# Routing in eleven slot-sized pieces, GpSimd work issued a slot later, input copies shared by two engines, and a regrouped end, in a gated cross-attention and mixture-of-experts kernel

## The chip, the cores and the metric

The kernel runs on one core of a Trainium2 chip. The core has five engines that work side by side, each through its own instructions in order: TensorE (PE in the profile) multiplies matrices, VectorE (DVE) and GpSimd (POOL) do elementwise work and reductions, ScalarE (ACT) does activations and copies, and SyncE (SP) issues most of the DMAs. They wait for one another through semaphores. The metric is the time of one execution on the device in microseconds (us), as the median of several runs. A profiled execution gives a trace of every instruction; its span runs from the first to the last instruction of the program.

## What is computed

```python
# x: 32 x 112 x 256, ctx: 32 x 375 x 256, all float32; 16 heads of 64; 8 experts, 2 of them per token
def attention(ctx, lat, ln_m_g, ln_m_b, ln_l_g, ln_l_b, Wq, Wkv, Wout):
    c = layer_norm(ctx, ln_m_g, ln_m_b)
    l = layer_norm(lat, ln_l_g, ln_l_b)
    q = l @ Wq                                        # 256 -> 1024
    k, v = split(concatenate([c, l], axis=1) @ Wkv)   # 487 keys
    attn = softmax(q @ k.T * 64 ** -0.5)              # for each batch and head
    return (attn @ v) @ Wout

def experts(x, gate_w, w1, b1, w2, b2):
    s, idx = top_k(softmax(x @ gate_w), 2); s = s / sum(s)
    y = gelu(x @ w1 + b1) @ w2 + b2                   # hidden size 1024, for each expert
    return sum over the two chosen experts of s * y

x = x + tanh(g_xattn) * attention(ctx, layernorm(x), ...)
x = x + tanh(g_ffn) * experts(layernorm(x), ...)
```

## The kernel before

**Attention, in 128 steps.** The 32 batches are taken in pairs. A step is one batch and two pairs of heads, so a pair of batches takes eight steps, m = 0 to 7; I call these eight a block, 0 to 15. Keys and values of a pair of batches come from a scheme of seven products instead of eight (`seven`, lines 341 to 418): four products (`p1`, `p6`, `p7`, `p5`) are copied from PSUM by ScalarE and summed by GpSimd (line 383), three more are added by VectorE (line 409).

A step n (lines 1034 to 1191) first runs `attend` of an earlier pair of steps on TensorE if n is even, then `scores(n + 1)` on TensorE with two maxima on VectorE (line 445, `nmx`), then five slots h = 0 to 4. In a slot TensorE gets one or two of the seven products or a query projection, then `turn_attn(n, h)` transposes a quarter of the attention weights, and VectorE copies it out of PSUM (line 481, `exT`). Behind that VectorE gets the slot's small work from a list `dve[h]`; the softmax's exponentials and its division (`exps`, `norm`) are on ScalarE, with a reciprocal on VectorE (line 468) before the division. All engines' orders are fixed by the order in which this Python code issues the instructions. PSUM banks for everything but scores come from a pool of four (`ps_m`), so TensorE runs at most four results ahead of the engines that empty them.

**What rides along.** Layer norm of a coming batch: statistics on VectorE (`stat`, line 218), roots on GpSimd (lines 237 to 246), application on ScalarE, all from `ln_parts`; then `turn` transposes the inputs on TensorE, and two ScalarE activations for each half copy them out with gain and offset (line 288), or VectorE does so for the first two batches (line 292). When a slab of 128 tokens is complete, `project`, `residual`, `normed` and `logits_of` give its output projection, residual sum, norm and eight gate logits (lines 517 to 569). Where a slab's number u is 0, these fall on steps m = 0, 2 and 3, where it is 1 on m = 0, 1, 4 and 5. Block 0 has no slab, the blocks 1, 5, 9 and 13 have one (u = 1), all others two.

**Routing.** Slabs form eight groups, six of four slabs and two of two. A step after a group's last logits, `route_parts` is issued: `first_choice` in slot 1, `second_choice` and `tanh` in slot 2, `counts` in slot 3; a step later `places` (two small matmuls into `ps_pos`, lines 629 and 632) in slot 0, with `gates`, and `slots_of` in slot 1. Then each token row is scattered to its expert's place in the table `xg` by indirect DMAs on GpSimd's queue (line 661), one a slot. For group 0, eight `stranger_hits` and `stranger_ids` come in between. Groups 0 to 5 end in the steps 27, 45, 61, 83, 99 and 117, group 6 in step 125, group 7 after the loop.

**Experts.** 60 blocks of 128 rows, which are fetched from `xg` in the order of the experts: `turn_rows` transposes, `hidden` is the first layer with Gelu on ScalarE, `second` the second layer, `combine` adds the bias on VectorE, scales, and scatters with addition on GpSimd's queue (line 910). The first ones run inside the last two steps and in the lines 1194 to 1238, from line 1256 on a plain loop. `locate_early` and `locate_late` compute on VectorE which rows each block takes.

## Time and profile before

| | before |
|---|---|
| median of 3 runs | 2220.05 us (2218.36 to 2221.41) |
| profiled execution | 2220.04 us |
| its span | 2218.3 us |
| TensorE busy | 2154.6 us |
| ScalarE, VectorE, GpSimd busy | 1296.7, 1229.0, 1015.3 us |
| mean granted TensorE clock | 0.991 |
| attention (first scores to last) | 20.1 to 1746.6 us |

A profile's line of a group or of the timeline gives start, duration, engine, source line, operation, what is written and read, shape, and in brackets the idle time before it and the instruction that ended it. TensorE's busy time includes small waits, as the ends of its pipelined matmuls are modelled; the distance between the starts of the same matmul in two steps does not have this fault.

### The profile page before, as it was taken

The numbers are of one execution on the slowest core, as the hardware profiler recorded it, in microseconds if no ns is written. First come the engines' busy times: TensorE is split into PE (matmuls) and PEld (weight loads), VectorE is DVE, ScalarE is ACT, GpSimd is POOL, SyncE is SP. The second block draws the span as 40 slices with busy tenths as digits, with TensorE's granted clock in tenths as the row PEclk, the third lists the DMA queues.
The fourth block names the chain that finished last, engine by engine and source line by source line (L and its number), as shares of the span: only waits on it lengthen the run. The fifth ranks groups of instructions, "written<-read, shape, count | busy, mean of one in ns | idle before, by whom it ended". The sixth has DMA issues, their size and how long they took to land. (4 is left out here: it accounts for less than half of the span.)

```text
span 2218.3 us, 42154 instructions
## 1 busy us (share of the span) xinstructions
PE 2154.6 (97%) x15944; PEld 1672.6 (75%) x15944; DVE 1229.0 (55%) x2698; ACT 1296.7 (58%) x3075; POOL 1015.3 (46%) x1388
## 2 busy tenths in 40 slices
PE   8999999999999999999999999999999899999998
PEld 5777767676777676777776777677767789999998
DVE  5566676767666767665667666756676541111111
ACT  5666666556666666667665666576655534344343
POOL 5745454455456544654545454555445232122122
PEclk9999999999999999999999999999999999999999
DMA  6592000010001000100000000000002236755453
GB/s 144 174 325 88 17 13 18 3 41 15 15 13 36 13 17 13 39 8 15 13 17 32 17 13 26 20 15 4 9 11 72 93 83 189 211 160 158 127 147 69
DMA packets 113701, 138.21 MB, mean 62 GB/s; under 512 B 14704, under 2 KB 101432, under 8 KB 113368
## 3 DMA queue, kind: packets, MB, share of 16 engines
q1 hardware_dynamic: 101032, 119.11, 17.3%
q0 software_dynamic: 11328, 15.33, 3.8%
q8 instruction: 127, 2.08, 0.4%
q10 hardware_dynamic: 1136, 1.05, 0.2%
q14 instruction: 78, 0.64, 0.1%
HBM read 166.84 MB, written 48.99 MB: 97 GB/s over the span
## 5 line engine op out<-in xcount | busy, mean ns | idle before, releaser
L470 ACT ACTIVATE ex<-ex,rc 112x487 f32<-112x487 f32 x512 | 331.7, 697 | 288.7 <-DVE rc L468 287.8
L445 DVE TENSOR_REDUCE nmx<-ps_s 112x2 f32<-112x974 f32 x256 | 287.3, 1163 | 346.3 <-PE ps_s L435 346.3
L456 ACT ACTIVATE ex<-ps_s,nmx 112x487 f32<-112x487 f32 x512 | 337.5, 667 | 167.5 <-DVE nmx L445 119.8
L481 DVE COPY exT<-ps_t 122x448 f32<-122x448 f32 x512 | 315.9, 617 | 105.8 <-PE ps_t L477 105.2
L477 PEld LDWEIGHTS ps_t<-ident,ex 112*122 112x122 f32 x2048 | 233.1, 139 | 138.5 <-issue 73.4
L887 ACT ACTIVATE h<-ps_h,b 128x128 f32<-128x128 f32 x480 | 175.6, 367 | 260.5 <-PE ps_h L880 220.1
L477 PE MATMUL ps_t<-ident,ex 112*122 112x112 f32 x2048 | 285.6, 262 | 17.7 <-ACT vv L403 7.3
L435 PE MATMUL ps_s<-kT,qT 64*112 64x487 f32 x1024 | 242.0, 591 | 0.0
L910 POOL DMA_INDIRECT out_dram<-y,xs x60 | 93.7, 1561 | 318.1 <-DVE y L909 189.2
L880 PE MATMUL ps_h<-xsT,w 128*128 128x128 f32 x1920 | 229.4, 277 | 4.8 <-ACT xsT L871 1.6
L880 PEld LDWEIGHTS ps_h<-xsT,w 128*128 128x128 f32 x1920 | 227.2, 194 | 9.1 <-issue 3.1
L491 PEld LDWEIGHTS ps_o<-exT,vv 122*64 122x64 f32 (+1 forms) x4096 | 197.7, 136 | 44.7 <-DVE rc L468 20.1
L893 PE MATMUL ps_y<-w,h 128*128 128x256 f32 x960 | 217.0, 379 | 0.0
L383 POOL TENSOR_TENSOR tmpv<-vv,tmpv 122x512 f32<-122x512 f32 x64 | 81.4, 1271 | 292.1 <-ACT tmpv L393 291.9
L491 PE MATMUL ps_o<-exT,vv 122*64 122x112 f32 (+1 forms) x4096 | 211.5, 260 | 0.0
L383 POOL TENSOR_TENSOR vv<-tmpv,vv 122x512 f32<-122x512 f32 x128 | 165.6, 1294 | 98.9 <-ACT vv L403 62.0
L373 PE MATMUL ps_v<-wkv_s,tT 128*122 128x128 f32 x1536 | 202.8, 275 | 0.2
L367 PE MATMUL ps_k<-tT,wkv_s 128*128 128x487 f32 x378 | 193.3, 594 | 4.7 <-ACT tmpk L393 3.2
L893 PEld LDWEIGHTS ps_y<-w,h 128*128 128x128 f32 x960 | 177.9, 190 | 21.8
L373 PEld LDWEIGHTS ps_v<-wkv_s,tT 128*122 128x122 f32 x1536 | 182.6, 186 | 2.2 <-issue 0.6
L373 PEld LDWEIGHTS ps_v<-wkv,kvT 128*122 128x122 f32 x1024 | 125.8, 185 | 74.3 <-issue 70.7
L409 DVE TENSOR_TENSOR kT<-ps_k,kT 128x487 f32<-128x487 f32 x189 | 124.8, 660 | 87.6 <-PE ps_k L367 80.1
(202 smaller groups left out, 3371.7 us busy)
## 6 DMA issues: line engine op xcount, KB each, us to landing
w<-in_L_ffn_w_dram SPq DMA_DIRECT2D x120, 1024.0 KB
xg<-pad SPq DMA_DIRECT2D x8, 3640.0 KB
cin<-in_ctx_dram SPq DMA_DIRECT2D x32, 336.0 KB
xs<-xg SPq DMA_DIRECT2D x60, 130.0 KB
b<-in_L_ffn_b_dram SPq DMA_DIRECT2D x60, 128.0 KB
xin<-in_x_dram SPq DMA_DIRECT2D x32, 112.0 KB
x<-in_x_dram SPq DMA_DIRECT2D x28, 128.0 KB
out_dram<-x SPq DMA_DIRECT2D x28, 128.0 KB
```

The lines of the kernel that those rows point to most:

```text
L367: nc.tensor.matmul(ps, lhsT=w[:, 0, i * P : (i + 1) * P], rhs=x[:, :NK], start=True, stop=True)
L373: nc.tensor.matmul(ps[:, c, :], lhsT=x[:, c * KC : (c + 1) * KC], rhs=w[:, 1, i * P : (i + 1) * P], start=True, stop=True,)
L383: nc.gpsimd.tensor_tensor(v[o], v[l], v[r], ALU.add)
L435: nc.tensor.matmul(ps[:, j, :NK], lhsT=qT[b // 2, i][r, b % 2, :], rhs=kT[b, i][r, :], start=True, stop=True,)
L445: nc.vector.tensor_reduce(nmx[b, i], pss[b, i][:, :, :NK], AX.X, ALU.max, negate=True)
L456: nc.scalar.activation(t[:, j, :NK], ps[:, j, :NK], AF.Exp, bias=nmx[b, i][:, j : j + 1], accum_out=sm[b, i][:, j : j + 1],)
L470: nc.scalar.mul(ex[b, i][:, j, :NK], ex[b, i][:, j, :NK], rc[:, j : j + 1])
L477: nc.tensor.transpose(ps[:, c, :], ex[b, i][:, j, c * KC : (c + 1) * KC], ident[:S, :S])
L481: nc.vector.tensor_copy(exT[b, i, j], ps)
L491: nc.tensor.matmul(ps[y * DH : (y + 1) * DH, r, x * S : (x + 1) * S], lhsT=vv[j][:m, c, x, r, y * DH : (y + 1) * DH], rhs=exT[2 * g + x, i ...
L880: nc.tensor.matmul(ps, lhsT=w1t[:, k, f * P : (f + 1) * P], rhs=xsT[t][:, k, :], start=(k == 0), stop=(k == KD - 1),)
L893: nc.tensor.matmul(psy[t], lhsT=hid[t][:, f, :], rhs=w2t[:, f, :], start=(f == 0), stop=(f == NF - 1),)
```

## The change

Routing becomes eleven parts (`choice` in six, `both`, `counts`, `places`, `gates`, `slots_of`), and from two slots after the last logits one part is issued in each slot. The `place` sum moves from `slots_of` to `gates`. GpSimd's roots and its copies of rows and token numbers are not issued at once but collected in `soon_` and issued after the next slot's `turn_attn`. The iota `slot` moves to another pool, and the four buffers of the exponentials become fixed tiles whose padding is zeroed once, not 256 times. Of the two halves of a turned input, ScalarE copies one out and VectorE the other. Batch statistics move from steps 7 and 1 to steps 6 and 7, and the application on ScalarE by one slot. At the start, weight sums are issued in another order. At the end the last products for K and V are spread over the steps 123 to 125 instead of 124 and 125, `turn_rows(0)` moves to the end of step 125 (and its copy to the pool `early`), the first hidden products of block 0 are cut otherwise, the counts are made a step later, and the order after the loop changes. Line numbers below are those of the text, not of the profile.

```diff
...
     wo_sb = wp.tile([P, NP, D], F32, name="wo_sb")
+    soon_ = []
+    outgoing = []
...
             stat(st[:S], mv[:S], CC, xin[b][:, 0, :])
+            soon_.append(roots)
+        def roots():
             gp = nc.gpsimd
...
+    exs = [[const.tile([S, 2, NKP], F32, name=f"ex_{n}_{p}") for p in range(2)] for n in range(2)]
+    for n in range(2):
+        for p in range(2):
+            nc.gpsimd.memset(exs[n][p][:, :, NK:], 0.0)
     def heads_of(n):
...
         ps = pss.pop((b, i))
-        t = soft.tile([S, 2, NKP], F32, tag="ex", name=f"ex_{b}_{i}", bufs=4)
-        nc.gpsimd.memset(t[:, :, NK:], 0.0)
+        t = exs[n % 2][p]
         sm[b, i] = soft.tile([S, 2], F32, tag="sm", name=f"sm_{b}_{i}", bufs=4)
...
         stat(st, mvx[i], 0, x1[i])
-        ve = small.tile([P, 1], F32, tag="vex", name=f"vex_{i}")
-        nc.gpsimd.tensor_scalar(ve, mvx[i][:, 0, 1:2], EPS, None, ALU.add)
-        rsx[i] = small.tile([P, 1], F32, tag="rsx", name=f"rsx_{i}")
-        nc.gpsimd.tensor_tensor(rsx[i], ve, nhalf[:, :1], ALU.pow)
+        def root():
+            ve = small.tile([P, 1], F32, tag="vex", name=f"vex_{i}")
+            nc.gpsimd.tensor_scalar(ve, mvx[i][:, 0, 1:2], EPS, None, ALU.add)
+            rsx[i] = small.tile([P, 1], F32, tag="rsx", name=f"rsx_{i}")
+            nc.gpsimd.tensor_tensor(rsx[i], ve, nhalf[:, :1], ALU.pow)
+        soon_.append(root)
...
         )
-        nc.gpsimd.tensor_copy(xr[g][:, j, 1, :D], xr[g][:, j, 0, :D])
+        soon_.append(lambda: nc.gpsimd.tensor_copy(xr[g][:, j, 1, :D], xr[g][:, j, 0, :D]))
...
-    def first_largest(src, n, g):
+    def first_largest(src, n, g, found):
         mx = rt.tile([P, src.shape[1]], F32, tag=f"mx{n}", name=f"mx{n}_{g}")
-        nc.vector.tensor_reduce(mx, src, AX.X, ALU.max)
         at = rt.tile([P, src.shape[1], E], F32, tag=f"sel{n}", name=f"sel{n}_{g}")
-        nc.vector.tensor_tensor(at, src, over_e(mx), ALU.is_equal)
-        nc.vector.tensor_tensor(at, at, over_b(rank, src.shape[1]), ALU.mult)
         top = rt.tile([P, src.shape[1]], F32, tag=f"top{n}", name=f"top{n}_{g}")
-        nc.vector.tensor_reduce(top, at, AX.X, ALU.max)
-        nc.vector.tensor_tensor(at, at, over_e(top), ALU.is_equal)
-        return mx, at
-    outgoing = []
+        found[f"m{n}"], found[f"s{n}"] = mx, at
+        def largest():
+            nc.vector.tensor_reduce(mx, src, AX.X, ALU.max)
+            nc.vector.tensor_tensor(at, src, over_e(mx), ALU.is_equal)
+        def where_first():
+            nc.vector.tensor_tensor(at, at, over_b(rank, src.shape[1]), ALU.mult)
+            nc.vector.tensor_reduce(top, at, AX.X, ALU.max)
+        def first():
+            nc.vector.tensor_tensor(at, at, over_e(top), ALU.is_equal)
+        return [largest, where_first, first]
...
-        def first_choice():
-            v["m1"], v["s1"] = first_largest(logits, 1, g)
-        def second_choice():
-            rest = new("rest", [P, RG, E])
-            nc.vector.scalar_tensor_tensor(rest, v["s1"], -BIG, logits, ALU.mult, ALU.add)
-            v["m2"], v["s2"] = first_largest(rest, 2, g)
+        choice = first_largest(logits, 1, g, v)
+        new("rest", [P, RG, E])
+        choice += first_largest(v["rest"], 2, g, v)
+        first, second = choice[2], choice[5]
+        def rest():
+            first()
+            nc.vector.scalar_tensor_tensor(
+                v["rest"], v["s1"], -BIG, logits, ALU.mult, ALU.add
+            )
+        def apart():
+            second()
...
+        choice[2], choice[5] = rest, apart
+        def both():
+            nc.scalar.activation(v["th"], v["th"], AF.Tanh, scale=0.5)
+            nc.vector.tensor_tensor(new("both", [P, RG, E]), v["s1"], v["s2"], ALU.add)
+            nc.vector.tensor_copy(new("had", [P, RG, E])[:, 0, :], macc)
         def counts():
-            both = new("both", [P, RG, E])
-            nc.vector.tensor_tensor(both, v["s1"], v["s2"], ALU.add)
-            had = new("had", [P, RG, E])
-            nc.vector.tensor_copy(had[:, 0, :], macc)
+            both, had = v["both"], v["had"]
             for j in range(1, RG):
...
-        def tanh():
-            nc.scalar.activation(v["th"], v["th"], AF.Tanh, scale=0.5)
         def gates():
+            place = new("place", [P, RG, E])
+            nc.vector.tensor_tensor(place, v["ps"], over_b(eoff, RG), ALU.add)
+            if g == 0:
+                strangers()
             half = new("half", [P, RG])
...
             for k in range(2):
-                nc.gpsimd.tensor_copy(
-                    xr[g][:, :, k, D + 1].bitcast(I32), tok[:, b0 : b0 + RG]
+                soon_.append(
+                    lambda k=k: nc.gpsimd.tensor_copy(
+                        xr[g][:, :, k, D + 1].bitcast(I32), tok[:, b0 : b0 + RG]
+                    )
                 )
...
         def slots_of():
-            place = new("place", [P, RG, E])
-            nc.vector.tensor_tensor(place, v["ps"], over_b(eoff, RG), ALU.add)
+            place = v["place"]
             slot = new("slot", [P, 2, RG])
...
-        pads = strangers, stranger_hits, stranger_ids, strangers_out
-        if g == 0:
-            return first_choice, second_choice, tanh, counts, places, gates, slots_of, pads
-        return first_choice, second_choice, tanh, counts, places, gates, slots_of
+        parts = choice + [both, counts, places, gates, slots_of]
+        return parts, (stranger_hits, stranger_ids, strangers_out)
...
-    (f0, t0), (f1, t1), (ln_now, ln_then) = (ln_parts(b) for b in range(3))
+    then = {}
+    (f0, t0), (f1, t1), (ln_now, then[2]) = (ln_parts(b) for b in range(3))
...
             part()
+    def now():
+        while soon_:
+            soon_.pop(0)()
...
     do(f0)
+    now()
     nc.vector.tensor_copy(lnT, ps)
...
         k_plain(0, i)
+    weight_sums(0, 1)
     do(f1)
-    weight_sums(0, 1)
+    now()
     do(t1)
...
     norm(0, 0)
-    weight_sums(1, 0)
+    do(ln_now)
+    now()
     ahead, behind = {}, {}
...
     do(ahead[0, 1][1:])
-    do(ln_now)
+    weight_sums(1, 0)
...
         none = [lambda: None] * 4
-        if n < LAST - 4:
-            one, two = ((1, jv), (0, jk))[odd], ((0, jk), (1, jv))[odd]
-            one, two = ahead.get(one, none), behind[two]
+        one, two = ((1, jv), (0, jk))[odd], ((0, jk), (1, jv))[odd]
+        one, two = ahead.get(one, none), behind.get(two, none)
+        if n < LAST - 5:
             slots = [[two[0], one[0]], [two[1]], [one[1], two[2]], [one[2]], [one[3]]]
...
-            slots = [[], [], [], [], []]
-            if n == LAST - 4:
-                for slot_, unit in zip(slots, behind[0, jk]):
-                    slot_.append(unit)
-            if n < LAST - 2:
-                j = LAST // 2 - 2 + odd
+            for j in (LAST // 2 - 2, LAST // 2 - 1):
                 if (1, j) not in ahead:
                     ahead[1, j], behind[1, j] = seven(1, j)
-                one, two = ahead[1, j], behind[1, j]
-                for slot_, units in zip(slots, (one[:2], one[2:3], one[3:], two[:2], two[2:])):
-                    slot_ += units
+            (p1, p6, p7, p5), (p2, p4, p3) = ahead[1, LAST // 2 - 2], behind[1, LAST // 2 - 2]
+            (q1, q6, q7, q5), (q2, q4, q3) = ahead[1, LAST // 2 - 1], behind[1, LAST // 2 - 1]
+            slots = {
+                5: [[two[0], one[0]], [two[1], one[1]], [two[2], p1], [one[2], p6], [one[3]]],
+                4: [[two[0], p7], [two[1], p5], [two[2], p2], [p4, q1], [p3, q6]],
+                3: [[q7], [q5], [q2], [q4], [q3]],
+            }.get(LAST - n, [[], [], [], [], []])
...
                 for h in range(4):
-                    dve[h].append(ln_then[h])
+                    dve[min(h + 1, 3)].append(then[nb + m // 2][h])
             if m == 1:
-                pe[1] += [lambda k=k: turn(nb, k) for k in range(KD)]
-                ln_now, ln_then = ln_parts(nb + 1)
+                pe[1] += [lambda: turn(nb, 0), lambda: turn(nb, 1, nc.vector)]
             if m == 3:
-                pe[1] += [lambda k=k: turn(nb + 1, k) for k in range(KD)]
+                pe[1] += [lambda: turn(nb + 1, 0), lambda: turn(nb + 1, 1, nc.vector)]
             if m == 4:
...
                     dve[h].append(part)
-            if m == 7 and nb + 2 < B:
-                ln_now, ln_then = ln_parts(nb + 2)
-            if m == 1 or (m == 7 and nb + 2 < B):
+            if m in (6, 7) and nb + 2 < B or n == 1:
+                u = m - 4 if m > 1 else 1
+                ln_now, then[nb + u] = ln_parts(nb + u)
                 for h in range(4):
...
             i = ended(2 * g - 2 + u) if g > 0 else None
-            if m == 6 + u and ended(2 * g + u) is not None and g + 1 < B // 2:
+            if m == 6 + u and ended(2 * g + u) is not None:
                 load_slab(ended(2 * g + u))
...
                 if group[i][1] == groups[group[i][0]] - 1:
-                    due, todo = n + 1, group[i][0]
-        if n == due:
-            r = route_parts(todo)
-            dve[1].append(r[0])
-            dve[2] += r[1:3]
-            dve[3].append(r[3])
-        if n == due + 1:
-            pe[0].append(r[4])
-            dve[0].append(r[5])
-            if todo > 0:
-                dve[1].append(r[6])
-            else:
-                far, hits, ids, ids_out = r[7]
-                dve[1].append(far)
-                at = [(j, e) for j in range(2) for e in range(0, E, 2)]
-                extra = [[lambda: None]]
-                for k in range(len(at) + 1):
-                    extra.append([lambda p=p: ids(*p) for p in at[k - 1 : k] if k > 0])
-                    extra[-1] += [lambda p=p: hits(*p) for p in at[k : k + 1]]
-                extra += [[ids_out], [r[6]]]
-        if n == LAST - 9:
+                    r, (hits, ids, ids_out) = route_parts(group[i][0])
+                    extra = [[], []] + [[part] for part in r[:10]]
+                    if group[i][0] == 0:
+                        at = [(j, e) for j in range(2) for e in range(0, E, 2)]
+                        for k in range(len(at) + 1):
+                            extra.append([lambda p=p: ids(*p) for p in at[k - 1 : k] if k > 0])
+                            extra[-1] += [lambda p=p: hits(*p) for p in at[k : k + 1]]
+                        extra.append([ids_out])
+                    extra.append(r[10:])
+        if n == LAST - 8:
             pe[0].append(lambda: found.update(ps=counted()))
...
             dve[1].append(lambda: next(early))
-        if n == LAST - 8:
+        if n == LAST - 7:
             for h in range(3):
...
             fetch_weights(0)
+        if n == LAST - 3:
+            pe[4].append(lambda: turn_rows(0))
         if n == LAST - 2:
-            pe[0] += [lambda: others(ends), lambda: turn_rows(0)]
-            pe[1] += [lambda: hidden(0, 0, 2)]
-            pe[2] += [lambda: hidden(0, 2, 4)]
-            pe[3].append(lambda: hidden(0, 4, 6))
-            pe[4] += [lambda: hidden(0, 6, 8), lambda: turn_rows(1, nc.scalar.copy)]
+            pe[0] += [lambda: others(ends), lambda: hidden(0, 0, 1)]
+            pe[1] += [lambda: hidden(0, 1, 3)]
+            pe[2] += [lambda: hidden(0, 3, 5)]
+            pe[3].append(lambda: hidden(0, 5, 7))
+            pe[4] += [lambda: hidden(0, 7, 8), lambda: turn_rows(1, nc.scalar.copy)]
         if n == LAST - 1:
...
             turn_attn(n, h)
+            then_ = soon_[:]
+            del soon_[:]
+            do(then_)
             for part in dve[h]:
...
     i, g = TS - 2, len(groups) - 1
-    while outgoing:
-        outgoing.pop(0)()
-    for u in range(2):
-        load_slab(i + u)
+    while extra:
+        do(extra.pop(0))
+    now()
+    do(outgoing)
+    del outgoing[:]
     attend(LAST // 2 - 1)
-    hidden(2, 0, 1)
+    hidden(2, 0, 2)
     for u in range(2):
...
     residual(i)
+    now()
     second(0)
     residual(i + 1)
+    now()
     normed(i)
-    hidden(2, 1, 2)
+    now()
+    logits_of(i, 0, 4)
+    hidden(2, 2, 8)
     normed(i + 1)
-    logits_of(i, 0, E)
+    now()
+    logits_of(i, 4, E)
     biased(0)
+    fetch_weights(3)
     logits_of(i + 1, 0, E)
-    fetch_weights(3)
-    first_choice, second_choice, tanh, counts, places, gates, slots_of = route_parts(g)
     turn_rows(3, nc.scalar.copy)
-    hidden(2, 2, 5)
-    first_choice()
-    second_choice()
-    tanh()
-    hidden(2, 5, 8)
-    counts()
+    r, _ = route_parts(g)
+    do(r[:7])
     second(1)
-    places()
+    fetch_weights(4)
+    r[7]()
+    second(2)
+    fetch_weights(5)
+    r[8]()
     found["ps"] = counted()
-    gates()
-    slots_of()
-    while outgoing:
-        outgoing.pop(0)()
+    r[9]()
+    now()
+    r[10]()
+    do(outgoing)
     locate_late()
...
     combine(1)
-    fetch_weights(4)
     for t in range(NE, NE + AHEAD):
...
     turn_rows(4)
-    second(2)
     combine(2)
-    fetch_weights(5)
...
```

More of the change, by code (lines that the diff above doesn't have):

```diff
@@ L138 @@
     nc.vector.tensor_copy(tokf, tok[:, :2])
-    slot = const.tile([P, P], F32, name="slot")
-    nc.gpsimd.iota(
-        slot, pattern=[[1, P]], base=0, channel_multiplier=0, allow_small_or_imprecise_dtypes=True
-    )
     row = const.tile([P, 1], F32, name="row")
@@ L192 @@
         b1rows = wqp.tile([E * NF, P], F32, name="b1rows")
+        slot = wqp.tile([P, P], F32, name="slot")
+        nc.gpsimd.iota(
+            slot,
+            pattern=[[1, P]],
+            base=0,
+            channel_multiplier=0,
+            allow_small_or_imprecise_dtypes=True,
+        )
         wq_sb = wqp.tile([P, KD, INNER], F32, name="wq_sb")
@@ L644, in gates @@
                 for k in range(2):
-                    nc.gpsimd.tensor_copy(
-                        xr[g][:, :, k, D + 1].bitcast(I32), tok[:, b0 : b0 + RG]
+                    soon_.append(
+                        lambda k=k: nc.gpsimd.tensor_copy(
+                            xr[g][:, :, k, D + 1].bitcast(I32), tok[:, b0 : b0 + RG]
+                        )
                     )
             def slots_of():
-                place = new("place", [P, RG, E])
-                nc.vector.tensor_tensor(place, v["ps"], over_b(eoff, RG), ALU.add)
+                place = v["place"]
                 slot = new("slot", [P, 2, RG])
@@ L869, in turn_rows @@
                 nc.tensor.transpose(ps[:, k, :], xs[t][:, k * P : (k + 1) * P], ident)
-            xsT[t] = found["tiles"].tile([P, KD, P], F32, tag="xsT", name=f"xsT_{t}")
+            xsT[t] = found["tiles" if t > 0 else "early"].tile(
+                [P, KD, P], F32, tag="xsT", name=f"xsT_{t}"
+            )
             (copy or nc.vector.tensor_copy)(xsT[t], ps)
@@ L1032 @@
         sums_at = {0: (0, 2), 1: (1, 1), 2: (0, 3), 3: (1, 2), 4: (0, 0), 5: (1, 3)}
-        filled, due, extra = 0, LAST, []
+        filled, extra = 0, []
         for n in range(LAST):
```

## The prediction

> **What bounds it now.** I read the page's busy shares first, then TensorE's windows block by block, its waits, and the timelines of the engines that it waits for.
>
> ```profile
> PE 2154.6 (97%) x15944; PEld 1672.6 (75%) x15944; DVE 1229.0 (55%) x2698; ACT 1296.7 (58%) x3075; POOL 1015.3 (46%) x1388
> ```
>
> TensorE has work 97% of the time and the change gives it none less. Only its waits, and the slow clock after them, can be won. The next windows cut the span at the first score matmul for each block of eight steps, which the step before it issues (columns: stretch, length, TensorE busy, granted clock, DMA share, GB/s); then come single steps.
>
> ```profile
> 220.92:327.94 107.02, 105.90 (x809) 1.00 0.05 15
> 327.94:447.61 119.67, 113.56 (x837) 0.97 0.03 10
> ...
> 992.18:1094.29 102.11, 101.61 (x793) 1.00 0.05 15
> 1094.29:1208.61 114.32, 109.31 (x814) 0.97 0.06 20
> ```
>
> ```profile
> 302.69:317.63 14.94, 14.45 (x125) 1.00 0.01 1
> ...
> 1176.90:1198.29 21.39, 17.45 (x129) 0.84 0.02 7
> ```
>
> A plain block takes 107.0 us (102.1 with one slab). Blocks with routing take more: block 3 12.65, 4 4.2, 6 5.5, 8 4.5, 10 7.3, 11 0.9, 12 7.1, 13 0.5; and step 119 7.1 more than its like (20.58 against 13.50). Sum 49.8. The pair of steps shows how: 6.45 us more, 3.45 of it idle and 3.4 (0.16 of 21.39) lost to a slow clock, less a little work.
>
> ```profile
> PE ps_pos L629 <- DVE had L619: 2.0, 1, 2.0
> PE ps_t L477 <- ACT vv L403: 1.4, 1, 1.4
> ```
>
> These are TensorE's waits around that step: the position matmul waits for the last instruction of `counts`, and a transpose for a PSUM bank that ScalarE frees late because it sat behind `tanh`. The timeline says why VectorE was late:
>
> ```profile
> 1177.79 1.21 POOL L322 TENSOR_TENSOR tT<-kvT 128x488 f32<-128x488 f32 x1
> 1177.91 1.14 DVE L583 TENSOR_TENSOR sel<-sel,rank 128x32 f32<-128x32 f32 x1
> ...
> 1180.42 1.27 POOL L383 TENSOR_TENSOR vv<-tmpv,vv 122x512 f32<-122x512 f32 x1 [1.42 <-ACT vv L398]
> 1180.47 1.49 DVE L560 CUSTOM_DVE_ANT_0 junk<-xr,gw_sb 128x256 f32<-128x256 f32 x1
> ```
>
> Alone, these two take 0.19 and 0.42 us; beside a GpSimd add they last as long as the add. Two more places, the start and the end:
>
> ```profile
> 37.51 0.60 ACT L250 ACTIVATE cin<-cin,sh,rsc 125x256 f32<-125x256 f32 x1 [3.72 <-POOL sh L246]
> 39.70 1.68 PE L367 MATMUL ps_k<-kvT,wkv_s 128*128 128x487 f32 x2 [3.29 <-ACT qT L306]
> ...
> 1751.61 1.28 ACT L887 ACT_TABLE_LOAD   x1
> ...
> 1775.72 0.96 POOL L661 DMA_INDIRECT xg<-xr,sloti  x1 [1.83 <-DMA xg<-xr,sloti]
> 1776.76 0.24 POOL L544 TENSOR_SCALAR vex<-mvx 128x1 f32<-128x1 f32 x1
> ...
> 1807.52 0.42 DVE L903 TENSOR_TENSOR y<-ps_y,b 128x256 f32<-128x256 f32 x1 [9.67 <-PE ps_y L893]
> ```
>
> Batch 2's shift comes late from GpSimd, ScalarE stands behind it, and TensorE 3.29 us behind ScalarE. At the end GpSimd computes slab 26's root only after four scatters.
>
> **What the Trainium skill says.** "SBUF — State Buffer", section "Who interferes with whom": a VectorE instruction with two SBUF inputs contends with a GpSimd instruction that reads SBUF, and the loser blocks wholly. The trace agrees (0.19 against 1.14 above). "TensorE: Matmul & The Clock Gate", "What's actually happening": an idle window of about 3.4 us halves the clock. The trace has half-clock stretches of 3.4 and 6.8 us, yet after single gaps of only 1.4 to 3.3 us. "ScalarE: Activation LUTs", "What ACT_TABLE_LOAD costs": 1283 ns a load; 1.28 here.
>
> **Routing, six groups in the loop.** What stays as work: `ps_pos` about 0.3 each, and eight pairs of `ps_ids` at 0.26, together 3.9. Removable: 49.8 - 3.9 = 46. What the pieces still cost:
> Groups 0, 3 and 4 end at step m=3, so four pieces (8 operations of 0.19 = 1.5 us) fall in m=4 beside logits. VectorE has gaps of 0.26 and 0.71 there, so 0.5 to 1.0 spills over. `both` and `counts` (6 at 0.17 = 1.0) fall in m=5, which without routing already loses 1.4 (14.94, against 13.54 for the same 124 matmul records in block 0, which has no logits), so they count in full. About nine operations have two SBUF inputs; with GpSimd busy 46% of the time I add one lost lock, 1.0. I take 3.0 each.
> Groups 1 and 2 end at m=5. Their pieces fall in m=6, where the change also puts batch statistics (four at 0.58 = 2.3). VectorE's gaps at m=6 are 0.26, 1.03, 0.75, 0.46 and 1.2 = 3.7 against 2.3 + 1.5, so that fits; m=7 has statistics and the 1.0 of `both` and `counts`: 1.5 each with half a lock.
> Group 5 likewise, without statistics: 0.5; but `locate_early`, a step later, puts seven operations (1.4) behind `residual` (1.1) in slot 0 of step 121: 2.5. Together 3.0.
> Group 0 also has eight `hit` comparisons (0.42 alone, 1.28 at most) in steps 30 to 32, beside statistics: 4.0 more.
> Left: 3 x 3 + 2 x 1.5 + 3 + 4 = 19. Gain **27**; bounds 12 (each piece meets an add) and 42 (none does). One part of the gain needs no gap: `ps_pos` held its bank of four until `slots_of`, for group 0 some twenty slots long, and now gives it back a slot later, at `place`.
> The scatters of a group, eight with two choices of four slabs, start three slots later and are no fewer; each still waits for the landing of the one before (about 2.9 us apart in the tail), and the adds queued behind them on GpSimd come late as now: step 87 loses 0.9 to that before, and I leave it.
> GpSimd's roots and row copies, a slot later: `normed` follows its root by four slots or more, the first application of a batch its roots by five, and the copies are read only by the scatters. No one waits: nothing.
>
> **Start.** Batch 2's roots go ahead of the K adds and its application a slot later: 3.29, and 1.7 for 3.4 us at half clock, go. `weight_sums(1, 0)` moves behind the K adds, where the second V product asks for it: +0.5. **-4.5** (bounds -2 and -5).
>
> **Steps 123 to 127.** TensorE's units there run 1.5, 0.5 and 3.1 us over their usual lengths in steps 123, 124 and 125. Spreading V's last fourteen products over three steps shortens the thinnest cover: I take 2 left, -3. `turn_rows(0)` ahead of the scores saves 1.3 behind the two `nmx` reductions. But `hidden(0, 0, 1)` now comes between two Exp groups: Gelu, Exp, Gelu, two more table loads, 2.57 us on ScalarE, which is busy almost throughout step 126 and frees the banks. +1 for 126 and 127. Together **-2** (bounds -5 and +3).
>
> **Tail.** Group 6's slots are ready at 1765.1 today, before the last attention; then, at its eleventh piece, about 3.9 us later. The four scatters hold GpSimd 10.8 us, each waiting for the one before, and slab 26's root is queued behind them: `normed(26)` about 2.4 later. From there VectorE's chain (sixteen logits at 0.47, routing) is the same, less a wait of 0.46, but `place` and the gates now precede the slots after the count matmul, +0.6. `second(2)` and `hidden(2, 2, 8)`, moved ahead, cover the 2.76 before `ps_pos`, but that wins nothing: `hidden(5)` starts when VectorE is free of the y at 1807.52, which waits for a buffer that GpSimd's first output scatter, behind four more scatters, releases. **+3** (bounds -3 and +5). `load_slab` and `fetch_weights(4)`, `(5)` go earlier on SP's queue; VectorE and TensorE wait for no such load here, so nothing.
>
> **Turned inputs, statistics, memsets.** Thirty pairs of copies leave ScalarE (1.00 a pair) for VectorE (0.97 a pair). At m=1 the statistics that leave (2.3) make room; at m=3 the copy falls in a gap of 1.18 after the second slot. Uncovered it would cost 29. I take **-0.5** for both (bounds -5, +15). The 252 memsets, 0.1 each, run in GpSimd's idle time, and Exp waits for `nmx` anyway: nothing.
>
> **Sum.** -27 - 4.5 - 2 + 3 - 0.5 = -31: span 2218.3 to 2187.3. The profiled execution took 2220.04, 1.7 more than its span, and equals the median 2220.05. Forecast 2189.
>
> **Rivals.** (B) The pieces vanish in VectorE's gaps and the tail does not slip: -42 - 4.5 - 3 + 2 = about -47, 2173. For: VectorE is 55% busy. Against: in odd steps it already decides. (C) The lock finds most pieces: routing -12, start -3, tail +3: 2208. For: half of the two-input operations in the step above were hit. Against: smaller lumps, and no position matmul directly behind them. (D) Slower: the 30 copies on VectorE. If exT and the reciprocals behind them reach TensorE late at m=1 and m=3, every pair costs 0.97: +29. With (A)'s gain of 31 that only cancels; beside (C)'s 12 it decides from 0.4 a pair on (30 x 0.4 = 12), and at 0.6 gives 2208 + 18 = 2226. Against: the gap of 1.18. (E) The gains and losses cancel, 2220.
>
> **How the numbers follow.** Chances: A 0.50, B 0.22, C 0.20, D 0.06, E 0.02. A's own range is 2181 to 2197. Ends at 2168 and 2210 take in most of B and C. No change is within 0.2%, 4.4 us, about what a measurement of this kernel can tell. A, B and C are faster: 0.92; E 0.02; D 0.06.
>
> **What would show it.** Blocks 6, 8, 10 and 12 within 1 to 4 us of 107; no wait of `ps_pos` for `had` near 2.0; plain blocks still at 107.0 (a shift of 1 us here moves the total by 15, and is what could make me most wrong); block 0 near 94, from 98.7; three table loads at step 126 where there is one; slab 26's root later than before against the last attention; and `hidden(5)` waiting for `y`.

## The result and the profile after

The changed kernel takes **2194.25 us** (median of four, 2192.12 to 2198.36) against 2219.66 for the kernel before (2218.36 to 2221.41): ratio 0.9887, 95% interval 0.987 to 0.9904, so 25.4 us less. The forecast was 2189, 31 less, with a range of 2168 to 2210. The profiled execution has a span of 2190.4 us against 2218.3, 27.9 less, and all sums below are made against that. It is the fastest of the four executions, so 2.5 of these 27.9 us go beyond what the medians show. The busy line of the page:

```profile
PE 2137.0 (98%) x15944; PEld 1663.3 (76%) x15944; DVE 1251.8 (57%) x2758; ACT 1271.5 (58%) x3017; POOL 1005.3 (46%) x1136
```

TensorE runs the same instructions, and the time it counts as busy falls by 17.6 us. It is not that work became less: matmuls at a slow clock after a stall, and small waits inside a group, count as busy. Only distances between the same matmuls show the whole. TensorE's windows, cut at the same score matmuls as in the prediction (stretch, length, busy, clock, DMA share, GB/s), first a plain block, then blocks 3 and 10 to 13:

```profile
215.22:322.10 106.88, 105.74 (x810) 1.00 0.05 15
322.10:435.96 113.86, 109.38 (x825) 0.99 0.05 15
...
1072.06:1182.37 110.31, 106.38 (x814) 1.00 0.06 16
1182.37:1291.24 108.87, 106.79 (x809) 1.00 0.08 24
1291.24:1400.84 109.60, 106.61 (x814) 1.00 0.05 15
1400.84:1508.11 107.27, 104.12 (x794) 0.98 0.06 18
```

Block 13 of the kernel before, for comparison:

```profile
1430.69:1533.28 102.59, 102.02 (x793) 1.00 0.05 14
```

Put beside the windows of before, this gives the whole account (after minus before):

| stretch | before | after | change |
|---|---|---|---|
| up to the first scores, and block 0 | 20.08 + 98.75 | 19.33 + 93.94 | -5.5 |
| six plain blocks (1, 2, 5, 7, 9, 14) | | | -1.0 |
| blocks 3 and 4 (group 0) | 230.93 | 223.48 | -7.5 |
| blocks 6 and 8 (groups 1, 2) | 224.13 | 215.79 | -8.3 |
| blocks 10 and 11 (group 3) | 222.22 | 219.18 | -3.0 |
| blocks 12 and 13 (group 4) | 216.77 | 216.86 | +0.1 |
| block 15 (group 5, and the last products) | 106.22 | 99.77 | -6.5 |
| from the last scores to the end | 471.74 | 475.61 | +3.9 |

A single row can be off by about 2 us: in the two runs below that change only the end, block 3 took 113.1 and 112.0 us against 113.9 here, and block 13 107.7 and 106.6 against 107.3.

Blocks 6 and 8 are within about one microsecond of a plain block, and step 119 has lost its stall (its interval is 14.15 us, 20.58 before). But block 13, which is 101.9 long when nothing disturbs it (as block 9 is), went from 102.59 to 107.27: the change made it slower. TensorE's waits say what is new:

```profile
PE ps_q L310 <- ACT vv L414: 11.2, 23, 2.7
PE ps_h L918 <- issue: 6.6, 3, 3.2
...
PE ps_t L492 <- ACT h L925: 3.2, 1, 3.2
...
PE ps_t L492 <- DVE kT L420: 2.3, 1, 2.3
```

The position matmuls' waits for `had` are gone, which were in the kernel before

```profile
PE ps_pos L629 <- DVE had L619: 6.0, 3, 2.0
```

and with them the 3.3 us wait of K's products at the start. In their place stand four others (of the same kinds the kernel before had no single wait above 1.2 us), each of which can be followed back.

**The wait of up to 2.7 for the query's bank** is the lock on VectorE, moved. This is the end of VectorE's work for step 84, where group 3's sixth piece shares slot 3 with two gate logits; TensorE is already in step 85:

```profile
1155.09 1.31 DVE L579 CUSTOM_DVE_ANT_0 junk<-xr,gw_sb 128x256 f32<-128x256 f32 x1
1156.08 1.44 POOL L394 TENSOR_TENSOR vv<-tmpv,vv 122x512 f32<-122x512 f32 x1
1156.33 1.25 DVE L613 TENSOR_TENSOR sel<-sel,top 128x32 f32<-128x32 f32 x1
1157.49 1.20 POOL L333 TENSOR_TENSOR tT<-kvT,tT 128x488 f32<-128x488 f32 x1
1157.50 1.22 DVE L644 TENSOR_TENSOR th<-mx,mx 128x4 f32<-128x4 f32 x1
1158.64 0.15 DVE L483 RECIPROCAL rc<-sm 112x2 f32<-112x2 f32 x1
1158.83 1.29 ACT L485 ACTIVATE ex<-ex,rc 112x487 f32<-112x487 f32 x2 [4.93 <-DVE rc L483]
1160.03 0.56 ACT L414 COPY vv<-ps_v 122x512 f32<-122x512 f32 x1
1160.64 1.02 PE L310 MATMUL ps_q<-kvT,wq_sb 128*128 128x224 f32 x4 [2.65 <-ACT vv L414]
```

Two operations that take 0.15 to 0.19 us alone take 1.25 and 1.22 beside GpSimd's adds, since each has two SBUF inputs and GpSimd's adds read SBUF too (the Trainium skill, "SBUF — State Buffer", "Who interferes with whom"; the trace agrees here as it did before). The logit ahead of them takes 1.31 where 0.42 is usual. The reciprocal is late, so ScalarE's division, so the copy behind it, so the PSUM bank, and TensorE stands 2.65 us, most of the 3.0 us that the three operations took too long. The chain has five links, and only the last shows in the list of waits.

The pieces are not locked less often than the lumps were: of group 3's 24 operations on VectorE four last over 0.8 us here, three before. What changed is where they fall, and that no position matmul waits for `had` right behind them. Two of the four (1.20 and 0.85 us, from 1139.15 and 1140.80) stand at the end of step 83, where VectorE then still waits 2.54 us for the scores, and they cost nothing: the interval is 15.81 us, as in a plain block.

**The wait of 2.3 for `kT`** is in block 13. GpSimd and TensorE, in order of time:

```profile
1411.39 1.09 POOL L699 DMA_INDIRECT xg<-xr,sloti  x1 [0.16 <-issue]
1415.85 0.96 POOL L699 DMA_INDIRECT xg<-xr,sloti  x1 [3.37 <-DMA xg<-xr,sloti]
...
1421.35 0.98 POOL L699 DMA_INDIRECT xg<-xr,sloti  x1 [0.57 <-DMA xg<-xr,sloti]
1422.37 1.22 POOL L394 TENSOR_TENSOR kT<-tmpk,kT 128x487 f32<-128x487 f32 x1
1423.66 1.21 POOL L394 TENSOR_TENSOR kT<-kT,kT 128x487 f32<-128x487 f32 x1
1424.90 0.67 DVE L420 TENSOR_TENSOR kT<-ps_k,kT 128x487 f32<-128x487 f32 x1 [4.63 <-POOL kT L394]
1425.62 0.85 PE L492 MATMUL ps_t<-ident,ex 112*122 112x112 f32 x4 [2.33 <-DVE kT L420]
```

The scatters, each waiting for the landing of the one before, now alternate with the K sums, and the last sum comes too late. Of the 5.3 us that block 13 has above block 9, 4.2 lie in the interval with this wait (17.98 against 13.77) and 1.1 in the one ahead of it, where the scatters already run.

**The other two** are at the end: a table load (ScalarE, step 126), and the turned rows of block 4, whose copy stands on VectorE behind `locate_late`:

```profile
1718.54 1.28 ACT L925 ACT_TABLE_LOAD   x1
...
1720.22 1.28 ACT L471 ACT_TABLE_LOAD   x1
...
1722.94 1.28 ACT L925 ACT_TABLE_LOAD   x1
...
1724.65 1.00 PE L492 MATMUL ps_t<-ident,ex 112*122 112x112 f32 x4 [3.24 <-ACT h L925]
```

```profile
1769.35 0.42 DVE L909 COPY xsT<-ps_x 128x256 f32<-128x256 f32 x1
...
1769.87 5.44 PE L918 MATMUL ps_h<-xsT,w 128*128 128x128 f32 x32 [3.24 <-issue]
```

In both cases the matmuls after the wait run at half clock for a while: four transposes 1.00 us where 0.55 is usual, 32 hidden products 5.44 where 3.73 is.

### The profile page after: what moved, and what is told of

It is laid out like the page before. It is cut to its first block, busy times and chain, and to the rows that moved or that the text cites. A ratio compares the mean times of both kernels' runs of the same rounds, so it can differ in the third digit from the quotient of the medians.

```text
span 2190.4 us, 41776 instructions
## 1 busy us (share of the span) xinstructions
PE 2137.0 (98%) x15944; PEld 1663.3 (76%) x15944; DVE 1251.8 (57%) x2758; ACT 1271.5 (58%) x3017; POOL 1005.3 (46%) x1136
## 3 DMA queue, kind: packets, MB, share of 16 engines
q10 hardware_dynamic: 1136, 1.05, 0.2%
## 5 line engine op out<-in xcount | busy, mean ns | idle before, releaser
L394 POOL TENSOR_TENSOR kT<-tmpk,kT 128x487 f32<-128x487 f32 x126 | 154.0, 1225 | 46.5 <-ACT kT L414 38.9
## 6 DMA issues: line engine op xcount, KB each, us to landing
xin<-in_x_dram SPq DMA_DIRECT2D x32, 112.0 KB
```

The source lines that it names most:

```text
L394: nc.gpsimd.tensor_tensor(v[o], v[l], v[r], ALU.add)
```

## The experiments

All start from the changed kernel. Where a length of a block is given, it is from the windows of that run's trace, cut in the same way.

### Routing in lumps again

```diff
-extra = [[], []] + [[part] for part in r[:10]]
+extra = [[]] * 5 + [r[:3], r[3:6], r[6:8], r[8:10]]
```

> The changed kernel with routing back in lumps: three parts of the first choice in slot 1 of the step after the last logits, three of the second in slot 2, both and counts in slot 3, places and gates a step later. All other edits stay. Theory A (the pieces themselves bring the gain of the blocks with routing, 23.9 us by their lengths in the two traces): blocks 3, 8, 10 and 12 back to about 119, 112, 114 and 114 us, step 119 back to about 20 us, and a time of 2212 to 2222. Rival (GpSimd's roots a slot later and the statistics in other steps made the room, and the cutting did little): less than 10 us lost, 2196 to 2204.

2215.17 us (2210.52 to 2220.85), ratio to before 0.9979 (0.9971 to 0.9987); span 2212.0. Blocks 10 and 12 are 114.5 and 114.4 again, block 3 118.2, blocks 6 and 8 110.8 each, the interval of step 119 17.4. So the cutting into pieces is worth about 21 us, and the rival as I put it (under 10 us) is out. But by the windows only 16.5 us of the loss lie in the blocks; 4.7 lie behind the last scores, where group 6's lumps fall. Lumps at their old places leave the blocks with routing, and step 119, some 7 us shorter than in the kernel before; that part is not the cutting's, and which other edit made it was not tried. Block 13 is 103.3 here: the lumps let the scatters start earlier, and what the pieces cost there is not paid.

### Roots at once

```diff
                 for part in dve[h]:
                     part()
+                    now()
...
                     do(extra.pop(0))
+                now()
```

> The changed kernel with GpSimd's roots and copies of rows issued at once again, not after the next slot's transposes. Theory: no one waits for them, so all blocks without routing keep their length within 0.1 us and the time stays within 2 us of 2194. Rival (the delay is what keeps GpSimd's adds on time): 0.3 to 1 us a block, 2199 or more.

2215.88 us (2209.05 to 2220.70), ratio 0.9982 (0.9973 to 0.999). I had given this edit nothing; undone, it costs 21.6 us, and every plain block 1.2 us (108.08). The first interval of a plain block, of which step m=7 is a part, went from 13.50 to 14.72. GpSimd and VectorE there:

```profile
216.99 1.27 POOL L394 TENSOR_TENSOR vv<-tmpv,vv 122x512 f32<-122x512 f32 x1
218.24 0.23 POOL L248 TENSOR_SCALAR vec<-mvc 125x3 f32<-125x3 f32 x1
...
221.12 0.19 POOL L257 TENSOR_TENSOR sh<-vec,rsc 112x1 f32<-112x1 f32 x1
221.26 1.27 POOL L394 TENSOR_TENSOR vv<-tmpv,vv 122x512 f32<-122x512 f32 x1
222.61 1.26 POOL L394 TENSOR_TENSOR vv<-vv 122x512 f32<-122x512 f32 x1
223.91 0.69 DVE L420 TENSOR_TENSOR vv<-ps_v,vv 122x512 f32<-122x512 f32 x1 [2.10 <-POOL vv L394]
```

Eight small operations, 3.0 us with their gaps, stand between the second and the third V add. Nobody waits for the roots; the adds queued behind them are what is late. In the changed kernel the same eight run from 220.13 on, behind the last V add, in time in which GpSimd is idle.

### Roots at once, and the statistics where they were

```diff
-if m in (6, 7) and nb + 2 < B or n == 1:
-    u = m - 4 if m > 1 else 1
+if m == 7 and nb + 2 < B or m == 1:
+    u = 2 if m == 7 else 1
```

with the edit of the run before.

> The changed kernel with the roots at once, as in the run that lost 22 us, and the batch statistics back in steps m=7 and m=1, as in the kernel before. Theory I (the delay of the roots pays for the move of the statistics: roots that are issued at m=6 stand between GpSimd's V adds and hold the last one back, and roots issued a slot later, or at m=7 and m=1, do not): plain blocks back from 108.1 to 106.9 to 107.1, blocks 6 and 8 from 111.8 and 112.8 to about 108 to 109.5, 2194 to 2200. Rival (the delay itself is what counts, whatever the statistics do): plain blocks stay at 108.1, 2213 to 2219.

2199.98 us (2196.25 to 2201.72), ratio 0.9909 (0.9892 to 0.9925). Plain blocks are 107.05 again: theory I holds, a delay of the roots is needed because the statistics now end at m=6. But blocks 6 and 8 stay at 110.8, above the 108 to 109.5 that I had given them. The excess, 2.55 us, has moved to the interval of step m=2 (12.86 against 10.31), where GpSimd runs a scatter, K sums, the eight operations of the roots at 698.80 to 701.91, another scatter, and only then the last two K sums. So the delay and the move of the statistics belong together: the move without the delay loses 15.9 us against having neither (2215.88 against 2199.98), both gain 5.7. The delay without the move was not tried.

### Scatters of groups 0, 3 and 4 eight slots later

```diff
+extra += [[]] * (8 * (1 - u))
 extra.append(r[10:])
```

> The changed kernel with only slots_of, and so the scatters, of groups 0, 3 and 4 eight slots later; the other ten pieces stay where they are. Theory S (in blocks 11 and 13 the scatters hold GpSimd, one behind the landing of the other, and its last K sums reach VectorE and TensorE late): block 13 from 107.3 to about 102, block 11 from 108.9 to about 107, blocks 3, 10 and 12 as they are (113.9, 110.3, 109.6): 2186 to 2189. Rival L (it is the lock on VectorE's pieces that is carried over from step to step, and scatters only happen to be there): blocks 11 and 13 within 1 us of now, 2193 to 2196.

2190.91 us (2189.74 to 2191.52), ratio 0.9867 (0.9851 to 0.9884). Blocks 10 to 13:

```profile
1076.24:1187.10 110.86, 107.47 (x813) 0.98 0.05 15
1187.10:1293.95 106.85, 105.74 (x810) 1.00 0.08 26
1293.95:1403.52 109.57, 106.59 (x814) 1.00 0.05 14
1403.52:1505.47 101.95, 101.45 (x794) 1.00 0.06 20
```

Theory S holds to the microsecond: blocks 11 and 13 lose nothing any more, 10 and 12 are as they were. The time gains only 3, less than I expected, because block 4 rises from 109.6 to 113.9: group 0's scatters, which come after its eight hit comparisons, now run in its steps m=3 to 5, and the intervals of these three steps are the ones that grew (by 2.0, 1.2 and 1.2).

### All pieces of these groups eight slots later

```diff
-extra = [[], []] + [[part] for part in r[:10]]
+extra = [[]] * (2 + 8 * (1 - u)) + [[part] for part in r[:10]]
```

> The changed kernel with all eleven pieces of groups 0, 3 and 4 eight slots later, so that they stand in steps m=5 to 7 as those of groups 1 and 2 do, which cost 1.0 us each. If both losses, the locked pieces beside gate logits at m=4 and the scatters, hang on the place alone, blocks 10 to 13 lose about 1 us a group: 110.3 to about 107.5, 108.9 to 107, 109.6 to 107.5, 107.3 to 102; with block 3 and 4 about 4 less, 2178 to 2184. Rival (statistics at m=6 and 7 take the room and the eight hit comparisons are what block 3 and 4 lose): a gain of 7 from the scatters alone, 2185 to 2189. Third: the later places meet the residuals of the next block, and nothing is won, 2192 or more.

2180.28 us (2179.84 to 2180.93), ratio 0.9822 (0.9806 to 0.9839), 14 less than the changed kernel, the first theory. Blocks 10 to 13:

```profile
1071.66:1178.51 106.85, 105.74 (x809) 1.00 0.05 15
1178.51:1286.40 107.89, 106.37 (x813) 1.00 0.08 25
1286.40:1393.26 106.86, 105.73 (x809) 1.00 0.05 14
1393.26:1496.23 102.97, 102.08 (x798) 1.00 0.07 20
```

A group costs 1.0 us, as groups 1 and 2 do. No operation was taken out. Against the changed kernel, blocks 10 to 13 are 11.5 us shorter: 6.8 of it came with the scatters' place in the run before, the other 4.7 with the pieces' place here, where no gate logits stand beside them. The lock is not gone: two of a group's 24 operations still last over 0.8 us (four and three in the changed kernel). Group 0 was the exception to my numbers: I expected about 4 from blocks 3 and 4, and they gave 1.3 (222.15 against 223.48), as block 4 holds 115.3.

### `hidden(0)` cut as before

```diff
-pe[0] += [lambda: others(ends), lambda: hidden(0, 0, 1)]
-pe[1] += [lambda: hidden(0, 1, 3)]
+pe[0] += [lambda: others(ends)]
+pe[1] += [lambda: hidden(0, 0, 2)]
...
```

> The changed kernel with hidden(0) cut in step 126 as before: two pieces of it in each of the slots 1 to 4, none in slot 0. Theory T (Gelu, Exp, Gelu: two more table loads and the wait of a transpose behind them): one table load is left in that stretch, the 3.24 us wait and the slow clock after it go, 4 to 6 us less, 2188 to 2190. Rival (the time is lost for other reasons, ScalarE is behind anyway): under 1.5 us less.

2187.01 us (2185.36 to 2189.61), ratio 0.9849 (0.9833 to 0.9866). The stretch from the last scores on takes 471.99 us instead of 475.61: 3.6 less. One table load is left, and a wait of 1.27 us stands in place of the 3.24. That is near theory T and below its 4 to 6; the medians differ by more, which the trace does not place.

### The copy of turned rows 4 on ScalarE, three y buffers

```diff
-turn_rows(4)
+turn_rows(4, nc.scalar.copy)
...
-ys[t] = found["tiles"].tile([P, D], F32, tag="y", name=f"y_{t}")
+ys[t] = found["tiles"].tile([P, D], F32, tag="y", name=f"y_{t}", bufs=3)
```

> The changed kernel with two edits behind the loop: the copy of turned rows 4 goes to ScalarE, so that hidden(4) does not wait behind VectorE's locating of blocks, and y has three buffers instead of two, so that VectorE's y of block 2 does not wait for the first output scatter. Theory: the 3.24 us and the 1.83 us in front of hidden(4) and hidden(5) go, with the slow clock 4 to 5 us from the last scores to the end, 475.6 to about 471. Rival (only passed on: the next scatter on GpSimd's queue holds the next y): under 1.5 us.

2186.79 us (2182.92 to 2191.97), ratio 0.9848 (0.9827 to 0.9868). The stretch is 472.87, 2.7 less, between theory and rival. The 3.24 us before hidden(4) shrink to 0.52, and the wait for y goes; but behind the next hidden products TensorE now waits 2.38 us for fetched rows (at 1781.26), and this run has a half-clock stretch of 3.41 us more ahead of the place of the edits (at 1731.45). The two edits were not tried apart.

### Both halves of a turned input on ScalarE

```diff
-pe[1] += [lambda: turn(nb, 0), lambda: turn(nb, 1, nc.vector)]
+pe[1] += [lambda k=k: turn(nb, k) for k in range(KD)]
```

and so for m=3.

> The changed kernel with both halves of a turned input copied by ScalarE again in steps m=1 and m=3. By the two traces each block with statistics is 0.18 us shorter in the interval that holds m=1, 2.6 in all, which I had put at 0.5 for the copies and the statistics together. Theory C (the copies: ScalarE frees banks earlier): the 0.18 comes back, 15 x 0.18 = 2.6, 2196 to 2198. Rival (the statistics that left m=1 are the cause): blocks as now, 2193 to 2195. Rival D of the prediction (30 copies on VectorE cost time, which other gains cover): faster than now by 5 or more.

2190.40 us (2188.97 to 2196.79), ratio 0.9872 (0.9853 to 0.9891), spans 2189.0 and 2190.4. The intervals with m=1 and m=3 are 14.45 and 15.80, as with the change (14.45, 15.81): the 30 copies are free on either engine. The medians differ by 3.9, which these intervals do not show. The 0.18 a block is not theirs. With the statistics back at m=1 the interval of m=1 is 14.63 to 14.64, so it is the statistics that left, the rival.

### Gate logits away from the V adds

```diff
 dve[0].append(lambda i=i: normed(i))
+dve[0].append(lambda i=i: logits_of(i, 0, 1))
 for h in range(1, 4):
-    dve[h].append(lambda h=h, i=i: logits_of(i, 2 * h - 2, 2 * h))
+    if h < 3:
+        dve[h].append(lambda h=h, i=i: logits_of(i, 2 * h - 1, 2 * h + 1))
...
-dve[0].append(lambda i=i: logits_of(i, 6, 8))
+behind_all.append(lambda i=i: logits_of(i, 5, 8))
...
 if h == 4:
+    do(behind_all)
     break
```

with the late pieces; up to step 119. The pieces of groups 1, 2 and 5 start two slots later.

> The pieces of groups 0, 3 and 4 late as in the earlier run, and besides the gate logits moved away from GpSimd's V adds: of a slab's eight, one directly behind its norm, two each in slots 1 and 2, and three at the end of the odd step behind slot 4, where VectorE waits 4.38 us for the scores; none in slot 3 of the even step nor in slot 0 of the odd one. Pieces of groups 1, 2 and 5 start two slots later. Theory G (these two places, locked with GpSimd, cost every plain block 0.76 and 1.4 us against block 0): intervals of 15.8 to about 15.1 and of 14.94 to about 13.6, plain blocks 106.85 to about 105, against the earlier run some 20 us less, about 2160. Rival (the three logits at the end of the step are locked with the K adds and hold the maxima back): nothing or a loss, 2179 to 2190.

2166.98 us (2166.09 to 2170.88), ratio 0.9764 (0.9748 to 0.9781). A plain block, and its intervals with m=3 and m=5:

```profile
214.46:319.25 104.79, 104.45 (x809) 1.00 0.05 16
```

```profile
269.94:284.28 14.34, 14.34 (x133) 1.00 0.00 1
294.59:308.94 14.35, 14.01 (x126) 1.00 0.00 1
```

15.81 and 14.97 became 14.34 and 14.35: 2.1 us in each block with two slabs that neither kernel had touched, as theory G had in sum, though I had given m=3 0.7 and m=5 1.3, and they gave 1.5 and 0.6. The lock itself is still there. VectorE at the end of the step m=3:

```profile
281.60 1.34 DVE L579 CUSTOM_DVE_ANT_0 junk<-xr,gw_sb 128x256 f32<-128x256 f32 x1
...
282.98 1.39 DVE L579 CUSTOM_DVE_ANT_0 junk<-xr,gw_sb 128x256 f32<-128x256 f32 x1
...
285.40 2.25 DVE L461 TENSOR_REDUCE nmx<-ps_s 112x2 f32<-112x974 f32 x2 [1.02 <-PE ps_s L451]
```

The moved logits last as long as GpSimd's K adds beside them, as the rival had it. Of a plain block's sixteen logits five last over 0.7 us, six in the changed kernel, and all sixteen together 11.4 us, 11.8 there. But they now fill a part of VectorE's 4.38 us wait for the scores, of which 1.02 us are left, and so hold nobody back.

The time stopped short of 2160 because block 15 rose to 109.6: group 5's scatters, two slots later, met the first fetch of rows in step 122, and GpSimd waited 7.05 us for that reading to end before it could write the table.

### All together

```diff
+if group[i][0] == 0:
+    extra += [[]] * 22
 extra.append(r[10:])
...
+if n < LAST - 16:
+    extra += [[part] for part in r[:10]]
+else:
+    extra += [r[k : k + 2] for k in range(0, 10, 2)]
```

and the edits of the runs with the logits, the cut and the tail.

> All that helped in one kernel: late pieces for groups 0, 3 and 4, gate logits away from the V adds, hidden(0) cut as before, turned rows 4 on ScalarE and three y buffers; besides, group 0's scatters 22 slots later (so that they fall at m=0 to 2, where those of groups 1 and 2 cost nothing), and the pieces of groups 5 and 6 in pairs, so that group 5's scatters end before the first rows are fetched in step 122 and do not wait for that reading (6.6 us on GpSimd in the changed kernel). Expected from the runs, in their traces: 2165.1, less 8 in block 4, 10 in block 15, 6 from the last scores on, 2141 of span, 2143. Rival (the edits hide one another's losses): 2155 or more.

**2145.66 us** (2143.56 to 2149.67), ratio to before 0.9671 (0.9655 to 0.9687): 74 us less than before and 49 less than the changed kernel, within 3 us of the sum of the parts. The windows of blocks 4 and 15:

```profile
423.98:533.83 109.85, 109.07 (x845) 1.00 0.06 14
...
1574.52:1675.09 100.57, 96.75 (x779) 1.00 0.15 46
```

Block 4 is 4.3 us shorter than with the logits alone (114.16), where I expected 8; block 15 is 9.0 shorter, where I expected 10; from the last scores on it is 10.0 shorter, where I expected 6. So the sum came out through misses that offset one another.

## Why the prediction was right, and where it was not

**The direction, the mechanism and the size.** Forecast a span of 2187.3, measured 2190.4; 31 forecast, 27.9 measured. By my own terms:

| term | forecast | measured |
|---|---|---|
| start | -4.5 | -5.5 (block 0: -4.8) |
| routing in the loop | -27 | -24.0 |
| steps 123 to 125 | -3 | 0 |
| step 126 and the end (+1 and +3) | +4 | +3.9 |
| turned inputs and statistics | -0.5 | -2.2 |

Routing is what the blocks and step 119 have above plain ones, 49.9 before and 25.9 after; the last row is what the plain blocks' own length makes; the others are stretches of the same windows. The total is nearer than its terms: the start and the last row gave 2.7 us more than forecast, routing and the steps 123 to 125 6.0 less. Of the start, 0.75 lies ahead of the first scores, a stretch that takes 19.1 to 20.4 in kernels that do not differ there, so it is no gain of the change.

**Routing.** I left 19 us and 3.9 of work in it, together 22.9; 25.9 are there. By groups: group 0 was put at 9.4 in all and took 9.7; groups 1 and 2 at 1.8 each, they took 1.0; group 5 at 3.3, it took 0.7; groups 3 and 4 at 3.3 each, they took 5.4 and 8.0. The failed step is the sentence on the scatters: they "start three slots later and are no fewer", and "the adds queued behind them on GpSimd come late as now", which I left at nothing. The shift moved them onto the K sums of the next block; by the run that moved only the scatters, this is 2.0 us in block 11 and 5.3 in block 13. I had the scatters' queue, their 2.9 us and the 0.9 that it already cost in step 87 on the page, and did not move them through the adds of the three slots. Of the locked operations I took one a group, 1.0 us. In group 3 the trace has two in a row behind a locked logit, and with no slack left on VectorE 2.65 of their 3.0 us reach TensorE through ScalarE and the bank; two more cost nothing, because VectorE waits there anyway. I had counted locks, and not asked where they fall.

**Nothing for the roots.** "No one waits: nothing" was right of the roots and wrong of the edit. I asked who waits for the roots' results, which is no one, and not what is queued behind them. The statistics moved to m=6, and with roots at once they would have stood before the V adds; the delay pays for that, 21.6 us of the time. Both together gain 5.7 us against neither, which I had not seen. That the forecast was not hurt is luck: I had priced neither the harm nor its cure.

**Steps 123 to 125.** I took 5.1 of loss there and left 2. The intervals of the steps 120 to 125 add up to the same before and after, within 0.1 us (those of 123 to 125 alone to 0.4 less); spreading the last products moved the loss from one step into another. GpSimd's wait of 6.59 us for the first fetch of rows is also in the changed kernel (at 1673.39), and I had not seen that a scatter there stands behind a reading. In the run with all edits, where group 5's scatters end before that fetch, the interval that begins in step 123 falls only from 16.35 to 15.84, so that wait is at most 0.5 of the 2.1 us by which this interval grew; the rest stays open.

**Step 126 and the tail.** Here the total was right by luck. The two more table loads were in the text at +1; undone, they give 3.6, for they delay a transpose by 3.24 us and the clock halves after it. The tail, +3, was so nearly 0 (3.9 - 3.6): slab 26's root does come 2.4 us later against the last attention (12.7 us behind it, 10.3 before), and hidden(5) waits 1.83 us for y, both as written. Against them stands the wait before `ps_pos` (2.76) with the 32 slow hidden products behind it (5.44 us), which are gone, and of which I wrote that their going "wins nothing"; that they balance is read from the two timelines and was not tried apart. What I missed is the wait for the turned rows of block 4: `second(2)`, moved ahead, had covered it; that copy on ScalarE, with a third y, gave 2.7.

**The rivals.** B failed at groups 0, 3 and 4, where about two thirds of the removable time stayed (20 of 30 us). C, where most of the gain stays away, came true for group 4 alone, and not by C's cause: there it is the scatters in block 13. D, the 30 copies on VectorE, is out: they cost nothing on either engine.

**What it said would show.** Blocks 6, 8, 10 and 12 at 107.9, 107.9, 110.3 and 109.6; block 0 at 93.94; plain blocks at 106.9; no wait for `had` of 2.0; three table loads; the late root; hidden(5) waiting. All seen.

## What to carry to other kernels

An edit that moves work on an in-order queue has two questions: who waits for its result, and what is queued behind it. The second was worth more here, twice: 21.6 us for roots that no one waited for, once the statistics had moved, and 7 us for scatters that were no fewer. A small vector operation is priced by where it stands: beside a GpSimd add it can last as long as the add, yet it cost TensorE nothing where VectorE was waiting for the scores anyway. So look for the stretch in which the operation's own engine waits, and put it there; cutting the work up was worth 21 us here without fewer operations being locked. And look at the steps that a change does not touch: the largest gain of the experiments, about 23 us over the blocks up to 14 (13 in that run's time, as block 15 lost 10), came with gate logits that the change had left alone.

## What the hardware did that I had not expected

The clock halves though TensorE is not idle for long. The Trainium skill ("TensorE: Matmul & The Clock Gate", "What's actually happening") gives an idle window of about 3.4 us for it. In the changed kernel the half-clock stretches, apart from one at the very end, begin at 412.07, 1425.83, 1722.79 and 1770.58 us, which are 297, 87 and 14 times 3.413 us apart, and in the 3.41 us ahead of each TensorE was still busy for 1.39, 1.08, 1.16 and 0.71 us. On the same grid of 3.41 us, windows with 1.58 us and more were followed by full clock. One of each (stretch, length, TensorE busy, clock, DMA share, GB/s):

```profile
1422.42:1425.83 3.41, 1.08 (x5) 1.00 0.11 39
1156.18:1159.59 3.41, 1.82 (x12) 1.00 0.00 0
```

So a stall of 2.65 us in block 3 was followed by half clock and the one of the same length in step 85 was not, because it fell across two windows (1.82 and 2.36 us busy). Over the other runs the border is less sharp: 2.26 us was followed by half clock in the run with the roots at once, 1.39 was not in the one with the copy of turned rows 4. A stall can thus cost more than its length: in block 13 four transposes took 0.85 us for 0.55 and eight V products 1.95 for 1.05, and the interval with the 2.33 us wait is 4.2 us too long.

A scatter into a table in DRAM waited 6.59 us, in another run 7.05, for a reading of that table by another queue, as each scatter waits for the landing of the one before. These are waits for semaphores, so the order is the program's; no run shows the chip without it. The scatters of the changed kernel mostly took 2.4 to 3.0 us from issue to landing, but eight of them 3.5 to 4.4 (one is that from 1411.39). Why is open.
